# The residual of the last group on VectorE, and a new order for the last two groups

## The chip, the cores and the metric

The kernel runs on one core of a Trainium2 chip. The metric is the time of one execution on the device in microseconds (us). Five engines work side by side, each through its own list of instructions in order: TensorE (PE), VectorE (DVE), ScalarE (ACT), GpSimd (POOL), and SyncE (SP), which here does nothing but issue transfers (DMAs). A batch is one of 128 matrices of 128 x 512 float32 numbers; they are worked on in 32 groups of four, so group 31 holds batches 124 to 127.

## The reference

Two layers act on every batch `x` (128 nodes, 512 features). The names are those of the reference; `adj` is 128 x 128.

```
x = layernorm(x + max_over_features(relu(adj @ x + b)))          # layer 0
q, k, v = split(x @ w_qkv)                                       # layer 1, 8 heads of 64
attn = softmax(where(adj == 0, -inf, q @ k.T / 8))
o = (attn @ v) @ w_proj + b_proj
ln = layernorm(o) * gamma + beta
x = layernorm(x + o + ln)
```

So the last normalization works on a sum of three things: the `x` that layer 0 left, `o`, and the normalized `o`. This sum is the residual of the title.

## The kernel before, in words

The work of a batch is cut into named steps, each a small function. In the order of the data:

- `load`, `conv`, `cmax`, `bn`, `ba`, `rstdx`, `shiftx`, `norm0` and their like are layer 0. What they leave of each batch, beside the normalized `x`, is a scale and a shift per row (`c0s[b]`), from which the same `x` can be made again out of the raw input.
- `xpl` (ACT) splits `x` into two 16-bit planes, `xrow` (SP) writes them to memory as `rowsx`, and `xcross` (SP) reads them back transposed as `xT`. `xmask`, `xsub`, `xhigh` and `xd` split `xT` into the three parts `x_h`, `x_l`, `x_d`.
- `dm` and `dd` (PE) are the dense products for q, k and v of a group: the main part (L810 and L811) and the correction (L816). `main` (ACT, L835) and `rest` (DVE, L839) carry them out of PSUM, the banks that PE writes to.
- `S` (PE, L856) makes the scores, `masked` (DVE, L870) adds the mask, `rmax` takes the row maximum, `exps` (ACT, L895) the exponentials, and `recip` and `wts` (DVE) divide by the sums. `pln`, `row` and `cross` bring the weights through memory to get them transposed (`eT`); for the last group `T` (PE, L929) and `wT` (ACT, L933) do that on the chip. `AV` (PE, L942) multiplies by v.
- `omask`, `osub`, `ohigh` and `od` split the result for `po` and `pod` (PE). For the last group `ocopy` (ACT, L983) and one plain product, `po` (PE, L992), stand in their place. `pmain` (DVE, L1005 for the last group, L1009 elsewhere) and `prest` bring `o` out of PSUM.
- `sq1` (ACT, L1042) sums the squares, `st1` (POOL, L1047 and L1048) makes the standard deviation's inverse, and `sm1` (POOL, L1051) the negative mean. `n1a` (DVE, L1063) and `n1b` (DVE, L1035) are the layer norm and the sum of the three things. `sq2`, `sm2`, `st2` (with L1080), `norm2` (ACT, L1084) and `out` (SP, L1087) are the last normalization and the store.

The residual has four steps. `res` (SP, L1022) loads the raw input again into `xb`; `resx` (POOL, L1025) makes the normalized `x` by scale and shift; `resb` (POOL, L1028) adds `beta`; `reso` (POOL, L1032) adds `o`. Then `n1b` reads `xb`. In the last group three of the four `reso` (batches 125, 126 and 127) already run on DVE, by the list `tail_vector`.

The order is not that of the loops. Tables give every step of every batch a place in time: `FIRST` for the first two groups, `STEADY` with a period of 55.3 us for the groups between, `LAST` for groups 30 and 31. All steps are sorted by place, and each engine's list is what this order leaves to it. `HOMES` gives every tile its buffer, a digit per group. An engine that reaches an instruction whose data or buffer isn't ready waits there, and all that stands behind it in its list waits too. SP's transfers wait in the same way.

Of the kernel before, what the change touches and what calls it, by code (L numbers as in the profile page):

```python
# [203 lines left out]
        'load': [-109.474, -114.726, -93.981, -90.742],  # L204
        'conv': [-104.237, -98.333, -82.773, -82.116],
        'cmax': [-101.892, -96.467, -82.184, -79.932],
        'relu': [-89.028, None, -76.607],
        'bn': [-102.389, -102.929],
        'ba': [-97.381, -99.226],
        'rstdx': [-91.240],  # L210
        'shiftx': [-88.508],
        'add0': [None, None, -74.236, -75.828],
        'sq0': [None, None, -66.957, -67.365],
        'rstd0': [None, None, -63.498],
        'shift0': [None, None, 287.249],
        'norm0': [-88.385, -87.588, -62.851, -60.493],
        'xpl': [-74.327, -86.981, -61.567, -54.001],
        'xrow': [-70.245, -80.244, -61.526, -46.314],
        'xcross': [-61.792, -51.026, -55.998, -43.528],
        'xmask': [-57.244, -41.596, -45.998, -35.427],  # L220
        'xsub': [-53.734, -36.213, -41.414, -33.891],
        'xhigh': [-49.203, -38.843, -38.848, -35.169],
        'xd': [-41.803, -28.755, -12.094, -25.033],
        'dm': [23.207, 11.124, 24.535, 28.796, -12.298, -32.939, -16.991, -33.689, -11.282, -21.144, -26.452, -22.965],
        'dd': [31.731, 30.191, 42.132, 24.720, -2.046, -3.233, -1.080, -2.017, -1.075, -11.713, -8.002, -8.311],
        'main': [23.965, 11.273, 28.136, 41.632, -10.613, -28.240, -12.184, -29.670, -5.627, -19.943, -7.194, -18.020],
        'rest': [35.642, 39.477, 48.794, 42.576, -1.794, -0.009, 2.750, -0.489, 1.324, -10.598, -4.784, -1.983],
        'S': [5.191, 7.896, 15.949, 36.535],
        'masked': [8.228, 9.789, 16.156, 55.632],
        'rmax': [23.382, 10.437, 23.419, 56.699],  # L230
        'exps': [32.521, 12.027, 45.923, 65.051],
        'recip': [38.371, 27.069, 48.649, 220.318],
        'wts': [61.926, 44.590, 53.940, 639.010],
        'pln': [74.229, 47.988, 55.572, 710.492],
        'row': [77.957, 50.229, 58.332, 756.534],
        'cross': [406.710, 53.366, 62.773, 1281.945],
        'AV': [527.077, 72.876, 470.794, 1552.458],
        'omask': [705.554, 168.484, 1395.316, 1861.627],
        'osub': [969.595, 195.060, 1430.151, 1869.293],
        'ohigh': [915.589, 295.545, 1470.100, 1979.426],  # L240
        'od': [1122.692, 433.988, 1860.884, 2301.225],
        'po': [1087.408, 432.513, 1779.318, 2195.782],
        'pod': [1128.757, 532.005, 2088.953, 2473.336],
        'pmain': [1475.008, 450.218, 1861.759, 2431.202],
        'prest': [1476.096, 706.452, 2171.852, 2518.007],
        'res': [62.370, 73.327, 1281.950, 1822.046],
        'resx': [910.657, 683.370, 1423.778, 2301.220],
        'resb': [1423.773, 937.413, 1573.982, 2381.062],
        'reso': [1663.460, 980.453, 2309.512, 2854.638],
        'sq1': [1528.274, 788.799, 2263.735, 2565.873],  # L250
        'sm1': [1771.504, 991.875, 2437.789, 3063.937],
        'st1': [1705.495, 969.978, 2311.415, 3001.611],
        'n1a': [1810.676, 1060.811, 2556.983, 3097.868],
        'n1b': [1811.771, 1186.462, 2669.560, 3144.253],
        'sq2': [1974.928, 1796.303, 2685.421, 3238.046],
        'sm2': [2097.450, 1222.877, 3004.293, 3164.575],
        'st2': [2239.253, 1958.774, 3063.658, 3309.867],
        'norm2': [2258.342, 1985.361, 3244.958, 3381.155],
        'out': [2943.922, 2451.194, 3934.517, 4169.894],
    },  # L260
    -1: {
        'load': [-144.215, -122.397, -87.832, -98.818],
        'conv': [-125.843, -113.821, -74.719, -73.132],
        'cmax': [-123.821, -111.010, -74.011, -70.007],
        'relu': [-105.209, None, -68.512],
        'bn': [-132.667, -119.140],
        'ba': [-113.535, -114.070],
        'rstdx': [-105.821],
        'shiftx': [-98.066],
        'add0': [None, None, -64.370, -64.409],  # L270
        'sq0': [None, None, -58.301, -56.762],
        'rstd0': [None, None, -56.284],
        'shift0': [None, None, 38.477],
        'norm0': [-97.506, -94.514, -53.295, -51.276],
        'xpl': [-91.979, -82.995, -53.005, -42.665],
        'xrow': [-87.966, -79.711, -46.343, -37.354],
        'xcross': [-85.577, -78.906, -40.869, -29.747],
        'xmask': [-53.264, -32.333, -15.235, -20.806],
        'xsub': [-28.786, -25.524, -13.495, -17.935],
        'xhigh': [-31.154, -31.299, -15.204, -18.122],  # L280
        'xd': [-13.832, -11.080, -0.231, -7.402],
        'dm': [1471.121, 1004.949, 1170.596, 1495.141, -1.773, -8.481, 6.077, -8.919, -6.615, 11.839, 6.299, 0.944],
        'dd': [1748.325, 1492.551, 1745.786, 1001.661, 101.381, 78.388, 17.350, 78.268, 285.621, 127.289, 152.999, 16.218],
        'main': [1642.360, 1334.960, 1490.846, 1913.034, 8.547, -5.208, 12.713, -2.155, -2.160, 17.532, 11.930, 1.614],
        'rest': [2513.844, 2222.373, 1815.474, 2223.252, 273.789, 171.234, 27.561, 134.230, 319.714, 223.386, 274.327, 89.444],
        'S': [568.110, 411.072, 408.806, 560.824],
        'masked': [899.659, 650.254, 639.949],
        'rmax': [1745.444, 994.197, 1359.490, 773.421],
        'exps': [1980.015, 1064.782, 1395.489, 816.797],
        'recip': [2293.717, 1427.228, 1745.745, 1131.177],  # L290
        'wts': [2297.099, 1749.082, 1906.226, 1371.032],
        'T': [2476.054, 2147.442, 2738.042, 2147.496],
        'wT': [2625.194, 2381.724, 2922.262, 2630.593],
        'AV': [2877.033, 2419.907, 3106.656, 2910.722],
        'lp': [1372.781, 1579.539, 775.912, 1383.693],
        'ocopy': [2944.230, 2625.101, 3364.788, 3210.244],
        'po': [3112.878, 2645.586, 3631.628, 3427.698],
        'pmain': [3309.789, 2821.443, 3713.225, 3475.853],
        'res': [2527.624, 1715.942, 2450.623, 2194.028],
        'resx': [3107.444, 2037.317, 3564.952, 3402.519],  # L300
        'resb': [3572.962, 2394.415, 3628.129, 3770.640],
        'reso': [3600.985, 3042.500, 3917.033, 4144.579],
        'sq1': [3327.687, 2832.513, 3861.424, 3835.253],
        'sm1': [3694.133, 3094.171, 3933.800, 3911.237],
        'st1': [3921.399, 3009.783, 4091.118, 3870.431],
        'n1a': [3711.006, 3115.652, 4022.948, 4287.614],
        'n1b': [4022.943, 3115.693, 4144.706, 4323.473],
        'sq2': [4032.619, 3203.386, 4423.644, 4431.735],
        'sm2': [4334.289, 3281.986, 4462.030, 4479.854],
        'st2': [4341.868, 3573.354, 4467.104, 4547.705],  # L310
        'norm2': [4572.886, 3831.270, 4578.057, 4810.017],
        'out': [4797.663, 4150.269, 4805.385, 5122.998],
# [27 lines left out]
    'first_h': [0, 0, 1, 0],  # L340
}
HOMES = {
    'adjx': '0',
    'adjp': '0',
    'wr': '10--110210201210',
    'xt': [
        '02100000000000000000000000000013',
        '10321321321321321321321321321331',
        '23213213213213213213213213213223',
        '31032132132132132132132132132102',  # L350
    ],
    'pa': [
        '11001200000000000000000000000031',
        '22231200000000000000000000000032',
        '02120333333333333333333333333303',
        '10210033333333333333333333333300',
    ],
    'xm': [
        '10011111111111111111111111111110',
        '01100000000000000000000000000011',  # L360
        '10110000000000000000000000000001',
        '10001111111111111111111111111111',
    ],
    'ptx': '3203',
    'cx': '01',
# [98 lines left out]
    ],  # L464
    'pod': [
        '',
        '3020000000000000000000000000230',
        '',
        '1111111111111111111111111110002',
    ],  # L470
# [10 lines left out]
def tile_adj_resnorm_d2(  # L481
# [12 lines left out]
    nc = tc.nc  # L494
# [681 lines left out]
```

## Time and profile before

| | before |
|---|---|
| median of 3 runs | 1835.1 us (1834.6 to 1837.3) |
| time of the profiled execution | 1834.2 us |
| span of the profiled execution | 1832.4 us, TensorE clock 0.996 |
| PE busy | 1802.5 us, 98% of the span |
| DVE busy | 1526.9 us, 83% |
| ACT busy | 1549.0 us, 85% |
| POOL busy | 1288.8 us, 70% |
| last matmul ends | 1818.5 us after the span's start |

The span runs from the first to the last instruction; the profiled execution's own time is 1.8 us longer. PE's busy time is an upper bound of its work, since matmuls are pipelined and their ends are modelled; what can be read surely is where PE was idle and what it waited for.

### The profile page before, as it was taken

How to read it: one execution, taken by the hardware profiler on the slowest of the kernel's cores; microseconds unless marked ns; L12 is line 12 of the kernel's file. 1: busy time of each engine (PE TensorE's matmuls, PEld its weight loads, DVE VectorE, ACT ScalarE, POOL GpSimd, SP SyncE). 2: the span in 40 equal slices, each digit the busy share in tenths (PEclk: the TensorE clock that was granted, in tenths of full speed). 3: DMA queues.
4: the chain of work that ended last, by engine and by line, in shares of the span. 5: the costliest groups of instructions: out<-in, count | busy, mean ns of one | idle time of the engine just before them, and what ended most of it. 6: DMA issues, size and time to landing. Idle time of an engine off the chain costs nothing.

```text
span 1832.4 us, 32628 instructions
## 1 busy us (share of the span) xinstructions
PE 1802.5 (98%) x10525; PEld 1420.9 (78%) x10525; DVE 1526.9 (83%) x2539; ACT 1549.0 (85%) x3959; POOL 1288.8 (70%) x1932
## 2 busy tenths in 40 slices
PE   7999999999999999999999999999999999999996
PEld 4777777788787778787788787887877787878874
DVE  7998887888887888888888888888888888888875
ACT  5898888888888888888888988888988888878875
POOL 4166567767767767777677777677677777768878
PEclk9999999999999999999999999999999999999998
DMA  5466666667666577656576756576666676556561
GB/s 162 135 165 178 174 161 156 167 160 201 173 165 164 157 178 192 176 157 160 165 186 174 181 147 169 160 202 173 165 167 159 173 197 178 159 152 185 138 156 69
DMA packets 486715, 303.95 MB, mean 166 GB/s; under 512 B 399504, under 2 KB 403728, under 8 KB 486544
## 3 DMA queue, kind: packets, MB, share of 16 engines
q1 hardware_dynamic: 485680, 300.75, 62.1%
q8 instruction: 83, 1.36, 0.3%
q10 hardware_dynamic: 864, 1.12, 0.2%
q14 instruction: 88, 0.72, 0.1%
HBM read 73.20 MB, written 131.07 MB: 111 GB/s over the span
## 4 chain that ended last, share of the span: by engine, by line
PE 86%; POOL 6%; DVE 3%; ACT 2%; issue 1%; DMA 1%; SPq 0%; POOLq 0%; ACTq 0%; DVEq 0%
PE psc L856 7%; PE pav L942 6%; PE pa L625 5%; POOL xb L1028 1%; POOL sum L1048 1%; POOL xb L1032 1%; ACT e L895 1%; DVE o L1035 1%; POOL x_d L742 1%; POOL od L742 1%; POOL xb L1025 1%; POOL sum L1051 0%; DVE o L1063 0%; POOL sum L1047 0%; PE pv L770 0%
## 5 line engine op out<-in xcount | busy, mean ns | idle before, releaser
L895 ACT ACTIVATE e<-e,nmax 128x128 f32<-128x128 f32 x1016 | 392.6, 392 | 2.5 <-DVE nmax L878 2.4
L742 POOL TENSOR_TENSOR od<-oh,ol 128x512 fp32r<-128x512 f32 x124 | 164.4, 1326 | 132.5 <-DVE ol L960 78.4
L910 ACT COPY planes<-e 128x2048 uint16<-128x2048 uint16 x124 | 234.8, 1893 | 9.8 <-DVE e L904 6.0
L1048 POOL TENSOR_TENSOR sum<-sum,mhalf 128x1 f32<-128x1 f32 (+1 forms) x287 | 217.3, 757 | 23.9
L1032 POOL TENSOR_TENSOR xb<-xb,o 128x512 f32<-128x512 f32 x125 | 165.3, 1322 | 53.1 <-DVE o L1035 50.7
L1042 ACT ACTIVATE squares<-o,sum 128x512 uint8<-128x512 f32 x256 | 183.2, 717 | 21.5 <-DVE o L1035 15.2
L895 ACT ACTIVATION_READ_ACCUMULATOR e<-e,nmax 128x1 f32 x1016 | 194.5, 191 | 0.0
L870 DVE SCALAR_TENSOR_TENSOR e<-psc,mask 128x1024 f32<-128x1024 f32 x127 | 152.3, 1218 | 42.7 <-PE psc L856 40.6
L1028 POOL TENSOR_TENSOR xb<-xb,beta_sb 128x512 f32<-128x512 f32 x128 | 165.9, 1296 | 2.9
L904 DVE TENSOR_TENSOR e<-e,sums 128x1024 f32<-128x1024 f32 x128 | 160.7, 1256 | 1.1
L1063 DVE SCALAR_TENSOR_TENSOR o<-o,sum,gamma_sb 128x512 f32<-128x512 f32 x128 | 101.3, 791 | 69.3 <-POOL sum L1051 61.2
L878 DVE TENSOR_REDUCE nmax<-e 128x8 f32<-128x1024 f32 x127 | 152.5, 1202 | 1.0
L736 POOL TENSOR_SCALAR oh<-oxh 128x512 fp32r<-128x512 f32 x31 | 64.9, 2093 | 117.0 <-DVE oxh L732 33.3
L709 ACT COPY xplanes<-xt 128x1024 uint16<-128x1024 uint16 x124 | 129.2, 1042 | 14.0 <-DMA rowsx<-xplanes 11.3
L856 PEld LDWEIGHTS psc<-qkT 64*128 64x128 f32 x2048 | 119.5, 188 | 19.1 <-issue 17.9
L625 PE MATMUL pa<-xt,adjT 128*128 128x512 f32 x256 | 132.5, 602 | 1.5 <-DVE rm L636 1.0
L856 PE MATMUL psc<-qkT 64*128 64x128 f32 x2048 | 132.3, 279 | 0.5 <-DVE o L1035 0.5
L942 PE MATMUL pav<-eT,v 128*64 128x128 f32 x2048 | 127.1, 276 | 0.9 <-ACT eT L933 0.8
L942 PEld LDWEIGHTS pav<-eT,v 128*64 128x64 f32 x2048 | 110.4, 137 | 18.0 <-issue 9.0
L1025 POOL TENSOR_SCALAR xb<-xb,sum 128x512 f32<-128x512 f32 x128 | 115.6, 904 | 9.3 <-DMA xb<-in_x_dram 9.2
L1035 DVE SCALAR_TENSOR_TENSOR o<-o,sum,xb 128x512 f32<-128x512 f32 x128 | 98.4, 769 | 23.2 <-POOL sum L1048 18.1
L697 ACT ACTIVATE xt<-xt,sum 128x512 f32<-128x512 f32 x128 | 103.8, 813 | 12.2 <-DMA wraw<-in_L_gnn_w_qkv_dram 6.1
(4263 smaller groups left out, 5507.6 us busy)
## 6 DMA issues: line engine op xcount, KB each, us to landing
rows<-planes SPq DMA_DIRECT2D x124, 512.0 KB, 3.1
xt<-in_x_dram SPq DMA_DIRECT2D x128, 256.0 KB, 3.1
xb<-in_x_dram SPq DMA_DIRECT2D x128, 256.0 KB, 2.8
out_dram<-o SPq DMA_DIRECT2D x128, 256.0 KB, 3.2
rowsx<-xplanes SPq DMA_DIRECT2D x124, 256.0 KB, 2.5
wraw<-in_L_gnn_w_qkv_dram SPq DMA_DIRECT2D x8, 256.0 KB, 3.1
xT<-rowsx SPq DMA_TRANSPOSE x124, 3.6
eT<-rows SPq DMA_TRANSPOSE x124, 4.9
```

The source lines that it names most:

```text
L625: nc.tensor.matmul(pa[b], adjT, xs[b], start=True, stop=True)
L742: engine.tensor_tensor(d, h.bitcast(FP), l.bitcast(FP), op=ALU.subtract)
L856: nc.tensor.matmul(psc[:, s, hp, :], qkT[hs, hp, i, :], qkT[hs, KC + hp, i, :], start=not with_mask, stop=not with_mask or hp == HP - 1,)
L878: nc.vector.tensor_reduce(nmaxs[b], es[b], AX.X, ALU.max, negate=True)
L895: nc.scalar.activation(es[b][:, j, :], src[:, j, :], AF.Exp, bias=nmax[:, j : j + 1], scale=by, accum_out=sums[b][:, j : j + 1],)
L904: nc.vector.tensor_tensor(es[b], es[b], sums.pop(b)[:, :, None].to_broadcast([P, H, P]), op=ALU.mult,)
L910: nc.scalar.copy(pl, es.pop(b).rearrange("p h m -> p (h m)").bitcast(U16).rearrange("p (m s) -> p s m", s=2),)
L942: nc.tensor.matmul(pavs[b][s * HD : (s + 1) * HD, hp, :], v[:, h * HD : (h + 1) * HD], eT[:, s * HP + hp, :], start=True, stop=True,)
L1028: nc.gpsimd.tensor_tensor(xbs[b], xbs[b], beta_sb, op=ALU.add)
L1032: engine.tensor_tensor(xbs[b], xbs[b], os[b], op=ALU.add)
L1042: nc.scalar.activation(junk[:, turn[0], :], src, AF.Square, bias=s[:, 0:1], scale=-float(D), accum_out=s[:, 1:2],)
L1048: nc.gpsimd.tensor_tensor(s, s, mhalf[:, :n], op=ALU.pow)
```

## The change

For the four batches of the last group, `resx` and `reso` become one DVE operation each of the form (in0 op scalar) op in1, and `resb` is dropped for all four: `beta` goes into the first operation in place of the shift, and the shift goes into the second beside `o`. So POOL loses four `resx`, four `resb` and one `reso`, and DVE gains four `resx` and one `reso` while its other three `reso` change their form. `tail_vector` no longer decides anything.

```diff
 TWO = {
...
     'tail_vector': [0, 1, 1, 1],
...
+    'tail_fused': [1, 1, 1, 1],
 }
...
+    def fused(b):
+        return bool(TWO["tail_fused"][b % G]) and b >= B - G
+
     def resx(b):
+        if fused(b):
+            nc.vector.scalar_tensor_tensor(
+                xbs[b], xbs[b], c0s[b][0], beta_sb, op0=ALU.mult, op1=ALU.add,
+            )
+            return
         nc.gpsimd.tensor_scalar(xbs[b], xbs[b], *c0s.pop(b), op0=ALU.mult, op1=ALU.add)
 
     def resb(b):
         nc.gpsimd.tensor_tensor(xbs[b], xbs[b], beta_sb, op=ALU.add)
 
     def reso(b, vector=False):
+        if fused(b):
+            nc.vector.scalar_tensor_tensor(
+                xbs[b], os[b], c0s.pop(b)[1], xbs[b], op0=ALU.add, op1=ALU.add,
+            )
+            return
         engine = nc.vector if vector else nc.gpsimd
         engine.tensor_tensor(xbs[b], xbs[b], os[b], op=ALU.add)
```

Beside this, both tables of `LAST` have new numbers throughout (the one of group 31 has no row for `resb` any more), and the digits of `HOMES` for groups 28 to 31 are partly new. The tables of the groups before are the same. No other step's work is changed. The built programs differ from the step `load` of batch 121 on. What the new numbers do to the engines' lists, where it is more than a neighbour changing places:

| list | in the old order | in the new order |
|---|---|---|
| PE, `conv` | 122 directly before 123 | 16 dense matmuls between 123 and 122 |
| PE, group 31 | `pd` 3, main part of product 1, `po` of 120, ..., main part of product 2 | main part of product 2, `po` of 120, `pd` 3, main part of product 1 |
| PE, `AV` of 122 | after `S` of 126 and 125 | before `po` of 121 and `S` of 125 and 126 |
| ACT, end | `wT` 125, `sq1` 123, `ocopy` 125, `wT` 124, `sq2` 122, `wT` 127, `sq1` 125, `wT` 126 | `wT` 125, `ocopy` 125, `wT` 127, `wT` 124, `sq2` 122, `sq1` 123, `sq1` 125, `wT` 126 |
| DVE, after the last matmul | `pmain` 126, `reso` 126, `n1b` 124, `n1a` 126, `reso` 127, `n1b` 126, `n1a` 127, `n1b` 127 | `pmain` 126, `n1a` 124, `reso` 126, `n1b` 124, `n1a` 126, `reso` 127, `n1b` 126, `n1a` 127, `n1b` 127 |
| ACT, `xpl` of 127 | directly after `exps` of 121 | after `sq2` 115, `ohigh` 118, `norm2` 115 and one `xhigh` |
| SP, `xrow` of 127 | before `res` of 116 and `out` of 115 | after them; `xcross` of 127 before that of 126 |
| SP, `xcross` of 125 | before `cross` of 117 | after `cross` of 119 and `res` of 117 |
| SP, `load` of 125 | after `row` of 113 | before `row` of 112 |

PE's last eight steps stand in the same order in both: `po` 125, `T` 126, `AV` 124, 127 and 126, then `po` 124, 127 and 126. So do SP's last thirteen transfers.

## The prediction

> **What bounds the kernel now.** I read the page's busy shares first, then the table by stretches of the end, then the waits of PE and the order of time at the end. The page says that PE is the bound, and which POOL groups the change touches:
>
> ```profile
> PE 1802.5 (98%) x10525; PEld 1420.9 (78%) x10525; DVE 1526.9 (83%) x2539; ACT 1549.0 (85%) x3959; POOL 1288.8 (70%) x1932
> ...
> L1032 POOL TENSOR_TENSOR xb<-xb,o 128x512 f32<-128x512 f32 x125 | 165.3, 1322 | 53.1 <-DVE o L1035 50.7
> ...
> L1028 POOL TENSOR_TENSOR xb<-xb,beta_sb 128x512 f32<-128x512 f32 x128 | 165.9, 1296 | 2.9
> ...
> L1025 POOL TENSOR_SCALAR xb<-xb,sum 128x512 f32<-128x512 f32 x128 | 115.6, 904 | 9.3 <-DMA xb<-in_x_dram 9.2
> ```
>
> The table by stretches (columns: from and to, length, busy us of PE, PEld, DVE, ACT, POOL; then clock and DMA) shows that POOL, 70% busy on average, is full at the end, while PE falls silent at 1818.5:
>
> ```profile
> 1790.00:1800.00 10.00, 9.94 (x67) 8.01 (x66) 7.76 (x14) 9.07 (x28) 9.51 (x15) 1.00 0.49 159
> 1800.00:1810.00 10.00, 9.17 (x69) 5.64 (x68) 8.00 (x13) 6.28 (x12) 9.25 (x16) 1.00 0.00 1
> 1810.00:1818.50 8.50, 8.50 (x20) 3.42 (x18) 2.34 (x5) 4.51 (x10) 8.17 (x13) 1.00 0.25 93
> 1818.50:1832.40 13.90, 0.02 (x1) 0.00 (x0) 6.21 (x13) 5.48 (x11) 8.89 (x21) 0.61 0.15 57
> ```
>
> So the end has two prices: idle time of PE before 1818.5, which moves everything, and the drain of 13.9 us after it. PE's waits from 1600 on, longest first:
>
> ```profile
> PE pp_(31, 1)_19690 L810 <- DVE e L870: 1.2, 1, 1.2
> PE pav L942 <- ACT eT L933: 0.8, 2, 0.5
> PE pa L625 <- DVE rm L636: 0.8, 1, 0.8
> PE pd_(31, 6)_19480 L816 <- ACT qkT L835: 0.7, 1, 0.7
> PE pm_(29, 6)_18211 L810 <- ACT qkT L835: 0.6, 1, 0.6
> PE pd_(28, 3)_18071 L816 <- DVE v L839: 0.3, 1, 0.3
> PE pm_(29, 8)_18196 L810 <- DVE qkT L839: 0.3, 1, 0.3
> PE pd_(31, 5)_19524 L816 <- DVE qkT L839: 0.2, 1, 0.2
> ```
>
> They sum to 4.9 us: all that a better order can win on PE. In the drain, DVE's order of time (start, length, instruction, idle before) shows two losses to POOL, an n1a of 1.73 us that delays pmain of 126, and an n1b that waits for POOL's statistics:
>
> ```profile
> 1817.56 1.73 DVE L1063 SCALAR_TENSOR_TENSOR o<-o,sum,gamma_sb 128x512 f32<-128x512 f32 x1 [1.67 <-POOL sum L1051]
> 1819.21 0.68 DVE L1005 SCALAR_TENSOR_TENSOR o<-pm_('o', 126)_20078,bias_sb 128x512 f32<-128x512 f32 x1
> ...
> 1821.65 0.75 DVE L1035 SCALAR_TENSOR_TENSOR o<-o,sum,xb 128x512 f32<-128x512 f32 x1 [1.02 <-POOL sum L1048]
> ```
>
> **What the Trainium skill says.** "GPSIMD Engine Reference", Engine selection, calls an elementwise operation with two inputs about twice as slow on GpSimd; here it is 1.30 us on POOL (L1028) against 0.69 (L1032 on DVE). "SBUF — State Buffer", Terms, says that DVE and GpSimd share a port pair held exclusively for a whole instruction. The trace agrees in kind only: the n1a above took 1.73 us beside a resb, and 0.75 at 1822.33, when POOL ran only operations of one column; but the 1.0 more is less than the 1.26 of that resb, so it wasn't shut out for all of it.
>
> **The change part by part.**
>
> *Work moved.* POOL loses 4 x 0.90 + 4 x 1.30 + 1.32 = 10.1 us, nearly all between 1790 and 1819. DVE gains five operations with a scalar per row, like n1b, at 0.77 (L1063 and L1035 mean 0.79 and 0.77): 3.9 us; three reso go from 0.60 to 0.68 start to start. DVE is idle 11 of the 40 us from 1780 to 1820, so this is hidden there; with that cover gone, it costs up to 3.9. Only the two reso behind pmain 126 lie on the end's path: 2 x 0.08 = 0.2. The new resx of 125 puts a wait for xb_125 into DVE's list, ahead of v's rest; its load was issued at 1780.9 and POOL's use was at 1790.5, so I take 0.
>
> *The drain.* P is the end of the last matmul. DVE, start to start: pmain 0.61, n1a 0.66, n1b and the new reso 0.68. In the new order: 0.1 + 0.61 + 3 x 0.66 + 4 x 0.68 + 0.75 puts the end of the last n1b at P + 6.2; before, it was 1825.8, P + 7.3. POOL: n1b of 124 ends at P + 2.8, its sq2 0.9 later; st2 of 124 takes 2.0, as at 1823.84, since DVE runs beside it: P + 5.7. sm2 and st2 of 126 and of 127 take 1.4 each, as from 1825.8 to 1828.6: P + 8.5. norm2 0.8 and the rest of the store 3.0 (1829.4 to 1832.4): P + 12.3 against P + 13.9, **1.6 us**. Bounds: 0.3, if DVE's chain is slowed to the old one, and 2.6, if st2 of 124 takes 1.1.
>
> *PE's waits from 1750 on.* The wait of 1.2 was for the scores' banks: product 1 needs two banks that masked of 124 frees. Now product 2, which needs one bank, goes first (1.8 us); masked of 124 ended 2.3 us after S of 124, so 0.5 of the wait stays: gain 0.7. The 0.8 for eT: ACT stood 3.0 us at sq2 of 122, with wT of 127 behind it, because n1a of 122 waited for POOL's queue (sm1 behind resb of 123). Now wT 127 and 124 come first: gain 0.8. The 0.7 and 0.2 are for banks that a main (ACT) and a rest (DVE) must empty; the pieces and bank digits are new there, and as every main stands ahead of its bank's next user by a product or more, I take both as gone: gain 0.9. Being earlier, PE meets the next one late: wT of 125 stands behind exps of 124 (3.1 us), oh_123 and norm2 of 121; counting from there it ends 0.4 after PE could start AV of 125: -0.4. Sum **2.0 us**, bounds -1.0 (other banks late instead) and 2.9.
>
> *PE's waits from 1600 to 1750.* conv of 122 no longer follows conv of 123 into a bank that cmax must free; 3.6 us of dense work lies between: 0.8. The 0.3, 0.6 and 0.3 sit where conv 124 and 125 move; I can't tell, and take -0.2 in sum for new ones: **0.6 us**, bounds -1.5 and 2.0.
>
> *Transfers moved past others.* load of 125 now waits for its buffer ahead of row 112; the transposed read of 112 stood at 1623.7 behind loads anyway, so 0. xcross of 125 now goes at about 1714.4 and, with 3.1 us to land, is there at 1717.5; its reader was at 1721.2: 3.7 spare. xpl of 127 would end at about 1722.6; rowsx lands 2.3 later, xcross of 127 then goes at 1724.9 and that of 126 at 1726.2, landing at 1729.3; its reader (xm) was at 1731.7: 2.4 spare. I take 0; without that cover each us late is a us of PE, since x_l of the last batch ended at 1734.7, just when PE began the dense products of group 31 (1734.4).
>
> Sum: 1.6 + 2.0 + 0.6 = **4.2 us**. The profiled execution took 1834.2 (span 1832.4, 1.8 around it) and would take 1830.0. The runs' median lies 0.9 above it, so for the median I give 1835.1 - 4.2 = **1830.9**.
>
> **The rivals.**
>
> *The waits only move.* PE waits only 4.9 of 233 us; an order that clears five waits may set five others, on banks and on ACT's mains. For it: the old order too has small waits everywhere. Against: each of the three largest has a named cause that is gone. Then only the drain gains: 1833.5.
>
> *DVE becomes the bound of the drain.* Nine operations stand behind the last matmul; if three more of them lengthen as the n1a above (1.0 each), the drain gains nothing. Against: POOL's long operations are gone by then. PE's gain of 2.6 stays: 1832.5.
>
> *Slower: the x of group 31 comes late.* xrow of 127 now stands in SP's list behind res of 116, which waits until n1b of 114 frees its buffer (in the old trace it went at 1720.3, at once after that n1b). The longest wait of this kind on SP was 8.5 us. So late, x comes 8.5 - 2.4 = 6.1 us after PE wants it, the gains of the order are lost with their timing, and only 1.6 remains: 1835.1 + 6.1 - 1.6 = 1839.6. It is slower from a lateness of 2.4 + 1.6 = 4.0 us on. Against it: that n1b stands in the new DVE list only one masked later.
>
> *It does not do what it says.* The built lists show nine instructions fewer on POOL and five more on DVE, so this is out.
>
> **How the numbers follow.** 0.2% is 3.7 us, about what a measurement of this kernel can tell from no change. Forecast 0.62 (0.54 of it beyond 3.7 us, as 4.2 is not far above), waits move 0.15, DVE bound 0.10 (0.02 of it beyond), x late 0.13 (0.10 slower by over 3.7, 0.03 less late). Faster 0.56, same 0.34, slower 0.10. The likeliest case alone spans 1828.2 to 1832.9. The sum of all the good bounds is 2.6 + 2.9 + 2.0 = 7.5, which gives 1827.6, and not all come together: 1828.2 below. Above, it takes in both middle rivals and the start of the slow one: 1836.0.
>
> **What would show it.** Right: the last matmul about 2.6 us earlier; no wait of DVE for sm1 (L1051) from 1790 on; no wait of pav for eT but one of up to 0.5 at 125; pp_(31, 1) without a wait; no n1a above 1 us in the last 15 us; a drain of 12 to 12.6 us. Wrong: new waits of PE before 1755, above all dense products of group 31 waiting for x_l or x_h; xm of 126 or 127 waiting for a DMA; a drain of 13.5 or more.

## The result and the profile after

The changed kernel took 1829.64 us (median of 8 runs, 1828.21 to 1832.19), the one before 1835.28 (8 runs): a ratio of 0.997, 95% interval 0.9959 to 0.998, so 5.6 us less where 4.2 were forecast. Timed a second time, beside other kernels of this study, it gave 0.9975 (0.9964 to 0.9986), 4.6 us less. The gain is real; whether it is larger than the forecast the times leave open, since both intervals (3.7 to 7.5 and 2.6 to 6.6 us) hold 4.2. One of the 13 executions of "changed, resx doubled" in the table below ran at a granted clock of 0.247, took 6970 us and is left out; all others ran at 0.995 or more. The profiled execution of the changed kernel took 1829.64 us, with a span of 1827.8.

From the page after: the busy shares, and the three POOL groups of the residual, which have lost the last four batches (x124 where they had 125 and 128):

```profile
PE 1801.2 (99%) x10525; PEld 1421.9 (78%) x10525; DVE 1528.4 (84%) x2544; ACT 1549.0 (85%) x3959; POOL 1283.9 (70%) x1923
...
L1045 POOL TENSOR_TENSOR xb<-xb,o 128x512 f32<-128x512 f32 x124 | 160.9, 1298 | 56.9 <-DVE o L1048 54.4
...
L1036 POOL TENSOR_TENSOR xb<-xb,beta_sb 128x512 f32<-128x512 f32 x124 | 163.7, 1320 | 2.7
...
L1033 POOL TENSOR_SCALAR xb<-xb,sum 128x512 f32<-128x512 f32 x124 | 114.8, 926 | 9.6 <-DMA xb<-in_x_dram 9.5
```

The table by stretches of the end (columns as in the prediction's). The last matmul now ends at 1815.42, and POOL, nearly full in the same place before, has room:

```profile
1790.00:1800.00 10.00, 9.89 (x62) 7.18 (x61) 8.54 (x15) 7.63 (x23) 8.91 (x10) 1.00 0.37 125
1800.00:1810.00 10.00, 9.76 (x70) 5.90 (x69) 6.25 (x15) 7.80 (x17) 7.45 (x17) 1.00 0.07 27
1810.00:1815.42 5.42, 5.42 (x13) 2.10 (x11) 2.71 (x6) 2.23 (x5) 2.88 (x7) 1.00 0.26 97
1815.42:1827.85 12.43, 0.00 (x0) 0.00 (x0) 6.12 (x13) 5.48 (x11) 6.82 (x16) 0.66 0.17 64
```

PE's waits from 1600 on, all of them:

```profile
PE pav L942 <- DMA eT<-rows: 0.8, 1, 0.8
PE pm_(29, 9)_18095 L810 <- ACT qkT L835: 0.4, 1, 0.4
PE pd_(28, 3)_18073 L816 <- ACT qkT L835: 0.4, 1, 0.4
PE pd_(31, 6)_19433 L816 <- ACT qkT L835: 0.3, 1, 0.3
PE pav L942 <- ACT eT L933: 0.2, 1, 0.2
PE pav L942 <- DVE ol L960: 0.2, 1, 0.2
```

They sum to 2.3 us against 4.9. The waits for `pp_(31, 1)` and for the convolution are gone, the one for eT is down to 0.2. A wait of 0.8 for a transfer of eT is new; in the second profile of the same kernel it was 0.4, so it varies from run to run. In the drain, VectorE's order of time has no pause above 0.05 us behind its first instruction and no long instruction any more (start, length, instruction):

```profile
1815.52 0.69 DVE L1005 SCALAR_TENSOR_TENSOR o<-pm_('o', 126)_20076,bias_sb 128x512 f32<-128x512 f32 x1 [1.41 <-PE pm_('o', 126)_20076 L992]
...
1816.14 0.75 DVE L1076 SCALAR_TENSOR_TENSOR o<-o,sum,gamma_sb 128x512 f32<-128x512 f32 x1
1816.80 0.75 DVE L1040 SCALAR_TENSOR_TENSOR xb<-o,sum,xb 128x512 f32<-128x512 f32 x1
1817.46 0.75 DVE L1048 SCALAR_TENSOR_TENSOR o<-o,sum,xb 128x512 f32<-128x512 f32 x1
...
1820.92 0.75 DVE L1048 SCALAR_TENSOR_TENSOR o<-o,sum,xb 128x512 f32<-128x512 f32 x1
```

**A ruler for what follows.** Two profiles can't be compared by their spans alone: single executions of one kernel lie over some 5 us, and ahead of the end the profile after ran 1.3 us later than that of before, in a part where the two programs are the same. So I split the end at marks read from the orders of time: A, from the start of the 113th instruction `masked` on VectorE (the first of group 28; the expectations call it batch 112's, it is 114's) to that of the last one, of batch 124; B, from there to the end of the last matmul; C, the drain. Before, the marks are 1595.20, 1774.38, 1818.52 and 1832.42; after, 1596.48, 1772.89, 1815.42 and 1827.85. Behind the last `masked` both have the same work for PE. One thing the marks do not share: in the four profiles of the old order the last `masked` starts 1.1 us after PE has ended its scores, in the ten of the new order 0.5 us after it (the reason is shown under the prediction's points). So between the two orders 0.6 us of what A falls belongs, for PE, to B. All kernels of this study:

| kernel | A | B | C | B + C | ratio to before (95%) |
|---|---|---|---|---|---|
| before | 179.2 | 44.1 | 13.9 | 58.0 | |
| changed, two profiles | 176.4, 175.7 | 42.5, 42.5 | 12.4, 12.4 | 55.0, 55.0 | 0.997 (0.9959 to 0.998), 0.9975 (0.9964 to 0.9986) |
| order alone, two | 176.3, 176.1 | 43.6, 43.6 | 15.3, 15.3 | 58.9, 59.0 | 1.0002 (0.9993 to 1.001), 0.9995 (0.9987 to 1.0003) |
| residual alone, two | 177.9, 179.4 | 44.8, 45.0 | 12.3, 12.3 | 57.2, 57.3 | 0.9997 (0.9988 to 1.0005), 0.9998 (0.999 to 1.0005) |
| order, only 125 fused | 177.1 | 42.9 | 15.5 | 58.4 | 0.9995 (0.9987 to 1.0004) |
| order, all but 125 fused | 176.3 | 43.6 | 12.4 | 56.0 | 0.9981 (0.9974 to 0.9988) |
| before, two waits attacked | 178.2 | 45.0 | 14.4 | 59.4 | 1.0007 (0.9999 to 1.0015) |
| changed, tail pulled | 175.2 | 42.5 | 11.5 | 54.0 | 0.9971 (0.9962 to 0.9981) |
| changed, tail ordered | 177.7 | 43.2 | 10.7 | 53.8 | 0.9966 (0.9954 to 0.9979) |
| changed, resx doubled | 178.1 | 44.0 | 12.4 | 56.5 | 0.9974 (0.9964 to 0.9984) |
| changed, reso doubled | 176.9 | 42.5 | 13.9 | 56.4 | 0.9977 (0.9969 to 0.9985) |

B + C repeats within about 0.1 us where a kernel was profiled twice; of before there is one profile. A varies by over 1 us: 177.9 to 179.4 in the four profiles of the old order (mean 178.7), 175.2 to 178.1 in the ten of the new one (mean 176.6). So the new order is worth about 2.1 us in A, with or without the new residual; 0.6 of them are the shift of the mark, and about 1.5 are PE's.

### The profile page after: what moved, and what is told of

Read it like the earlier page. It is cut to its first block, busy times and chain, and to the rows that moved or that the text cites. A ratio compares the mean times of both kernels' runs of the same rounds, so it can differ in the third digit from the quotient of the medians.

```text
span 1827.8 us, 32614 instructions
## 1 busy us (share of the span) xinstructions
PE 1801.2 (99%) x10525; PEld 1421.9 (78%) x10525; DVE 1528.4 (84%) x2544; ACT 1549.0 (85%) x3959; POOL 1283.9 (70%) x1923
## 5 line engine op out<-in xcount | busy, mean ns | idle before, releaser
L1055 ACT ACTIVATE squares<-o,sum 128x512 uint8<-128x512 f32 x256 | 183.1, 717 | 21.8 <-DVE o L1048 15.8
L1045 POOL TENSOR_TENSOR xb<-xb,o 128x512 f32<-128x512 f32 x124 | 160.9, 1298 | 56.9 <-DVE o L1048 54.4
L904 DVE TENSOR_TENSOR e<-e,sums 128x1024 f32<-128x1024 f32 x128 | 159.9, 1250 | 1.1
L1076 DVE SCALAR_TENSOR_TENSOR o<-o,sum,gamma_sb 128x512 f32<-128x512 f32 x128 | 99.2, 775 | 64.3 <-POOL sum L1064 57.2
L709 ACT COPY xplanes<-xt 128x1024 uint16<-128x1024 uint16 x124 | 129.2, 1042 | 14.4 <-DMA rowsx<-xplanes 12.2
L697 ACT ACTIVATE xt<-xt,sum 128x512 f32<-128x512 f32 x128 | 103.9, 813 | 12.4 <-POOL sum L691 10.0
```

The lines of the kernel that those rows point to most:

```text
L904: nc.vector.tensor_tensor(es[b], es[b], sums.pop(b)[:, :, None].to_broadcast([P, H, P]), op=ALU.mult,)
L1045: engine.tensor_tensor(xbs[b], xbs[b], os[b], op=ALU.add)
L1055: nc.scalar.activation(junk[:, turn[0], :], src, AF.Square, bias=s[:, 0:1], scale=-float(D), accum_out=s[:, 1:2],)
```

## The experiments

### The two halves alone

Order alone: the tables and homes of the changed kernel, the residual of before.

```
-    'tail_fused': [1, 1, 1, 1],
+    'tail_fused': [0, 0, 0, 0],
...
         'resx': [3353.537, 2093.860, 3785.974, 3547.076],
+        'resb': [3353.541, 2093.865, 3785.976, 3547.080],
```

> The new order with the old residual: the tables and homes of after, with the last four batches' residual as before (resx and resb on GpSimd, resb put directly behind resx; reso on GpSimd for 124, on VectorE for the other three). My theory, two parts that add: PE keeps its part (last matmul about 4.4 us earlier than before, counted from the masked instruction of batch 112), but the drain is as before or longer, 13.9 to 14.5 us against 12.4 in after, because POOL again has four operations of 0.9 and four of 1.3 between the statistics: about 1831.3 us, 1.7 above after. Rival, the order gives everything: 1829.6, as after. Rival, the relief of POOL gives most: 1834 or more, with DVE waiting for POOL's sm1 and PE waiting again before 1815.

Residual alone: the tables and homes of before, with the new functions.

```
+    'tail_fused': [1, 1, 1, 1],
...
-        'resb': [3572.962, 2394.415, 3628.129, 3770.640],
```

> The new residual in the old order: the tables and homes of before without the row resb of the last group, and the fused resx and reso on VectorE. My theory: PE waits as before (four or five waits, 4 to 5 us from 1600 on, pp_(31, 1) and pav for eT among them), the drain falls from 13.9 to 12.4 to 12.9 us, because n1a of 124 no longer waits for POOL's queue and no longer lasts 1.73 us: about 1834.0 us, 1.3 less than before. Rival, the order gives everything: 1835.3. Rival, the relief of POOL gives most: 1831.5 or less, with the waits of PE after 1790 gone too.

Each was timed twice. The expectations of the second time:

> The order alone, a second time. The times said 0.1 us more than before, the trace said 2.0 less (PE's stretch 3.4 shorter, drain 1.4 longer). If the trace stands for the kernel, the ratio is about 0.999 (1833.1) and PE's stretch is again 218 to 220.5; if the times do, 1.000 and a stretch nearer 222. The waits of 0.6 at pd_(o, 123) for POOL's od and of 0.7 at pav for eT, and a drain of about 15.4, should come back in either case.

> The residual alone, a second time: ratio 0.9992 (1833.5), since the drain is 1.5 us shorter (12.3 to 12.4) and PE's stretch is that of the old order, 222.7 to 223.3. If the times of the first measurement were right at 0.9 us less, the same within their error.

Neither half showed what I expected of it. The order alone was 0.4 us slower and 0.9 faster than before (ratios times 1835) where I expected 4.0 faster; the residual alone was 0.6 and 0.4 faster where I expected 1.3, which its intervals still hold. No interval leaves 1 out. The changed kernel is 5.5 and 4.6 faster. My theory of two parts that add is refuted by the order alone, and so is the rival that the order gives everything. The rival that the relief of POOL gives most was right for the order alone (1834 or more, with PE waiting again) and wrong for the residual alone (1831.5 or less). Of the second expectations, the order alone met that of its trace (PE's stretch A + B 219.7, both waits back); the residual alone had a stretch of 224.3, longer than the 222.7 to 223.3 expected.

B + C and A together show where the two parts interlock. In B + C, from 58.0, the residual alone takes 0.8, the order alone adds 0.9, and both together take 3.1; A's 2.1 for the order come on top. This makes 0.8 for the residual, 1.2 for the order and 5.2 for both. That fits the times but for the order alone, which they put at 0.3 on average. Of this difference 0.2 lies outside the span (its executions took 2.0 us around the span, those of before 1.8); the rest is within what A's spread allows and was not settled.

What holds the order back shows in its waits. From the view of PE's waits of the order alone, from 1773 on:

```profile
PE pav L943 <- ACT eT L934: 0.7, 1, 0.7
PE pd_('o', 123)_19922 L817 <- POOL od L743: 0.6, 1, 0.6
```

and from its order of time on VectorE at the end:

```profile
1815.68 0.69 DVE L1006 SCALAR_TENSOR_TENSOR o<-pm_('o', 127)_20068,bias_sb 128x512 f32<-128x512 f32 x1 [3.79 <-DMA out_dram<-o]
...
1819.15 0.69 DVE L1006 SCALAR_TENSOR_TENSOR o<-pm_('o', 126)_20080,bias_sb 128x512 f32<-128x512 f32 x1 [2.77 <-DMA out_dram<-o]
...
1822.47 0.75 DVE L1049 SCALAR_TENSOR_TENSOR o<-o,sum,xb 128x512 f32<-128x512 f32 x1 [1.35 <-POOL sum L1062]
```

The last matmul ended at 1817.96, but pmain of 126 started 1.2 us later (0.1 in the changed kernel), because the buffer of `o` that it writes was still being stored: with POOL's statistics behind the residual, norm2 and the stores of the earlier batches are late (the last two norm2 ahead of the last matmul's end started 5.3 and 1.8 us before it, 6.7 and 4.8 in the changed kernel). And n1b waits another 1.35 for POOL. This makes the drain 15.3.

### Which batch's residual costs what

From the changed kernel; the diff is that of the first run, and the second has the flags 1, 0, 1, 1 and a place of `resb` for 125 alone.

```
-    'tail_fused': [1, 1, 1, 1],
+    'tail_fused': [0, 1, 0, 0],
...
+        'resb': [3353.541, None, 3785.976, 3547.080],
```

> The new order; the new residual for batch 125 alone, the other three as before on GpSimd. In the order alone, PE waited 0.6 us at pd_(o, 123) for od of 123, which stood on POOL behind resb of 125 (2.1 us), and the drain was 15.3. Theory: the parts interlock at two places, POOL ahead of 1800 (batch 125, PE's part) and POOL behind 1808 (124, 126, 127, the drain). Then PE's stretch from the masked instruction of batch 112 to the last matmul falls from 219.9 to about 219 us, and the drain stays at 15 or so: about 1.0 us less than the order alone. Rival, only the amount of POOL's work counts: both fall a little, the drain to about 14.5.

> The counterpart: the new order; the new residual for 124, 126 and 127, batch 125 as before on GpSimd. Theory: PE's stretch as in the order alone, 219.9 us with its wait of 0.6 at pd_(o, 123), and the drain as in the changed kernel, 12.4: about 1.0 us above the changed kernel. Rival, only the amount counts: PE's stretch 219.2, drain 13.1.

The changed kernel ran beside them:

> The changed kernel again, unchanged, beside the next three on one chip. The order alone and the residual alone, timed together, gave 0.1 more and 0.9 us less than before; the change as a whole had given 5.6 less in another session. If the two parts need each other, it gives 5 to 6 less here too: 1829.6. If that figure owed something to its session, 2 to 3 less.

It gave 4.6 less (by the ratio), between the two branches of its expectation and nearer the first. The theory of two places holds in B and C. In A + B the run with 125 alone fused missed it (220.0 where about 219 was expected), with a wait of 1.9 us in A, at `po` of 118 for an n1b, that no other profile has. With 125 on GpSimd the drain is that of the changed kernel (12.4), and PE's waits behind the last `masked` are again just these two:

```profile
PE pav L943 <- ACT eT L934: 0.7, 1, 0.7
PE pd_('o', 123)_19922 L817 <- POOL od L743: 0.6, 1, 0.6
```

With 125 alone fused the second is gone, the first falls to 0.2, and the drain stays at 15.5. So batch 125's two POOL operations cost PE 1.1 us (B, 43.6 against 42.5). Both waits come out of POOL's list. The od of 123 stands behind the two operations: it ended 21.8 us after the start of the last `masked` in the order alone, 20.0 after it in the changed kernel. And the last wT stands on ACT behind squares that wait for an n1b, whose n1a waits for POOL's reso: with 125 on GpSimd that n1b came 1.2 us later than in the changed kernel. The operations of 124, 126 and 127 cost 2.9 to 3.1 us of drain, and with 125 alone fused B is still 42.9, as `po` of 126 starts 0.4 late behind ACT's oxh. The rival, that only the amount counts, gave a drain between the two in both runs; neither showed one.

### What sets the drain

Changed kernel, order of the end alone: `st1` of 124 behind its `sm1`; `n1a`, `n1b` of 124 (and in the second run `reso`, `n1a` of 127) ahead of pmain of 126; resx of 126, the statistics, squares, norm2 and stores are moved along. The diff is of the first version and cut to two rows; the second has n1a of 127 at 3812.600.

```
-        'n1a': [3877.907, 3291.580, 4309.470, 4559.968],
+        'n1a': [3812.400, 3291.580, 3850.000, 3840.000],
-        'n1b': [4302.225, 3324.051, 4356.434, 4579.296],
+        'n1b': [3812.420, 3324.051, 3851.000, 3842.000],
...
```

> After, with only the end of the order changed: st1 of 124 directly behind sm1 of 124 on POOL, and n1a, reso and n1b of 124 behind pmain of 127 on VectorE, so that six of its operations stand behind the last matmul instead of nine; statistics, squares, norm2 and stores follow in the order 124, 127, 126. If VectorE's chain behind the last matmul sets the drain, as the prediction's sum has it, the last n1b comes about 1.5 us earlier (last matmul + 4.7 instead of + 6.25) and the drain falls from 12.4 to about 10.9 us: 1828.1 us. If POOL's chain of statistics or the stores set it, the drain stays at 12 to 12.4: 1829.6. If the n1a of 124 holds up pmain of 127 or 126, it is longer.

In this first version reso of 124 and 127 read `o` after n1a had overwritten it, so for these two batches another residual is added; the instructions are as many and as long. The second version keeps the arithmetic:

> The changed kernel with a shorter drain, by order alone and with the same arithmetic: st1 of 124 behind its sm1 on POOL; on VectorE reso of 124 ahead of pmain of 127, then n1a and n1b of 124, reso and n1a of 127, so that only pmain of 126, n1b of 127, reso, n1a and n1b of 126 stand behind the last matmul, five operations in place of nine. If VectorE's chain sets the drain: last n1b at about last matmul + 4.0, drain 10.2 to 11.0 us against 12.4, and about 1.5 to 2 us less than the changed kernel, 1827.8. If POOL's statistics of 126 or the stores do, the drain stays above 11.8.

And the reverse, two more operations behind the last matmul:

```
+            if b >= B - 2:
+                nc.vector.scalar_tensor_tensor(
+                    xbs[b], xbs[b], 1.0, beta_sb, op0=ALU.mult, op1=ALU.add,
+                )
```

> The changed kernel with a second operation of the same form behind the fused reso of 126 and of 127 (it adds beta once more): two more of VectorE's operations behind the last matmul, eleven instead of nine. If VectorE's chain sets the drain, it grows by 2 x 0.66 = 1.3 us to 13.7 and the last n1b comes at last matmul + 7.6. If POOL's chain has slack or sets it, the drain grows by less than 0.7.

In the changed kernel VectorE's chain sets it, and POOL's statistics run level with it. Two operations more made the drain 13.9, 1.45 longer (0.73 each), with the last n1b ending 7.7 us after the last matmul instead of 6.25. In the first version two fewer, not three, stand behind the last matmul (seven; the expectation counted six): the drain was 11.5, 0.95 shorter. In the second, four fewer made it 10.7, 1.76 shorter, and the last n1b came 1.76 earlier too. That is less than four times 0.68: pmain of 126 starts 0.26 late behind n1a of 127, n1a of 126 pauses 0.13 behind its own reso, and the last n1b waits for the next limit, POOL's st1 of 126 (VectorE's order of time of the tail ordered):

```profile
1819.17 0.75 DVE L1048 SCALAR_TENSOR_TENSOR o<-o,sum,xb 128x512 f32<-128x512 f32 x1 [0.46 <-POOL sum L1061]
```

Both orders also take statistics of 124 on POOL out of the drain. That POOL has to be shortened along with VectorE shows in the residual alone. Its VectorE chain ends 5.7 us after the last matmul, 0.5 sooner than in the changed kernel, and the drain is 12.3 all the same: there POOL's statistics run with no pause above 0.1 us from 0.9 after the last matmul to the last st2, 8.5 after it.

The tail ordered has the lowest ratio of the study, 0.9966 against 0.9975 of the changed kernel beside it; the intervals overlap, so that it is the better one is shown by its drain, not by the times. Its B was 0.6 longer, with waits of pav for eT of 0.7 in sum that the edit wasn't to touch; their cause stays open.

### Is VectorE's added work hidden?

```
             nc.vector.scalar_tensor_tensor(
                 xbs[b], xbs[b], c0s[b][0], beta_sb, op0=ALU.mult, op1=ALU.add,
             )
+            nc.vector.scalar_tensor_tensor(
+                xbs[b], xbs[b], 1.0, beta_sb, op0=ALU.mult, op1=ALU.add,
+            )
```

> The changed kernel with a second operation of the same form behind each of the four fused resx on VectorE (it adds beta once more): 4 x 0.68 to 0.75, about 2.8 us more on VectorE, all ahead of the last pmain. The prediction took VectorE's five added operations as hidden. If so, no change: the drain stays at 12.4 us and PE's stretch from the masked instruction of batch 112 to the last matmul stays within what its repeats show, 217.7 to 220.9; time as the changed kernel, 1830 to 1831. If VectorE has no slack there, up to 2.8 us more, with PE waiting for VectorE behind 1790.

Only partly. C is unchanged, but B grew from 42.5 to 44.0, and PE's waits behind the last `masked` name VectorE:

```profile
PE ppt L929 <- DVE o L1051: 1.0, 1, 1.0
PE ppt L929 <- DVE e L904: 0.5, 1, 0.5
```

They sum to the 1.5. So the slack there is about half of the 2.8 us added. (PE's stretch A + B was 222.2, above the 220.9 that the expectation allowed; the rest of that lies in A.) The times (4.8 less than before, as the changed kernel) can't tell 1.5 us.

The residual alone points the same way in the old order: its B is 0.7 to 0.8 longer than before's, with a new wait of 1.2 of `pm_('o', 125)` for ACT's oxh. The traces show what held that oxh up. The new resx of 125 puts a `wts` (L904) on VectorE 0.7 us later, and this changes which of two operations starts first, it or a reso on POOL. Before, then the residual alone:

```profile
1795.28 1.22 DVE L904 TENSOR_TENSOR e<-e,sums 128x1024 f32<-128x1024 f32 x1
1795.33 2.32 POOL L1032 TENSOR_TENSOR xb<-xb,o 128x512 f32<-128x512 f32 x1
```

```profile
1792.58 1.28 POOL L1045 TENSOR_TENSOR xb<-xb,o 128x512 f32<-128x512 f32 x1
1792.84 2.10 DVE L904 TENSOR_TENSOR e<-e,sums 128x1024 f32<-128x1024 f32 x1
```

Before, VectorE was 0.05 us ahead and POOL's reso lasted 2.32; now POOL was ahead and `wts` lasted 2.10 instead of 1.22. So 0.7 us of added work became 1.6 us at pmain of 123, 1.4 at the prest of 123 behind it (counted from the last `masked`), and `sq1` of 123, which waits for that, stands ahead of `ocopy` of 125 on ACT.

### Two waits taken out of the old order

```
-        'dm': [1471.121, 1004.949, 1170.596, 1495.141, ...],
+        'dm': [1471.121, 1170.596, 1004.949, 1495.141, ...],
...
-        'wT': [2625.194, 2381.724, 2922.262, 2630.593],
+        'wT': [2625.194, 2381.724, 2922.262, 2629.000],
```

> Before, with two small edits of its order and nothing else: product 2 of group 31 changes places with product 1 (so the one that needs a single bank comes first), and wT of 127 goes ahead of sq2 of 122 on ACT. They aim at the two longest waits of PE at the end, 1.2 us at pp_(31, 1) and 0.8 at pav for eT. If each wait costs what the view of waits shows less the 0.5 that I left standing, the time falls by 1.5 us to 1833.8; if a wait costs PE more than its idle time (start to start, those places stood 1.39 and 1.27 us above the usual pace), by 2.0 to 2.6: 1833.0. Rival, the waits only move: 1835.3, with new waits of the same sum in the view of waits.

The rival was right here, and the loss was larger still in the profile: B grew by 0.9 and the drain by 0.5. From its waits of PE, from 1776 on:

```profile
PE pp_('o', 120)_19700 L810 <- POOL od L742: 1.4, 1, 1.4
PE pav L942 <- ACT v L835: 0.9, 1, 0.9
PE pav L942 <- ACT eT L933: 0.7, 2, 0.4
```

The wait of `pp_(31, 1)` went, and `po` of 120, now straight behind product 2, waited 1.4 for od of 120 in its place. The two for eT stayed at 0.7 in sum, and one for v came. With these two edits alone the waits moved; the new order took `pp_(31, 1)` out and left 0.2 for eT by moving the rest as well (`pd` 3 now stands behind the main part of `po` 120, for one).

## Why the prediction was right, point by point

**Drain, 1.6 forecast: 1.5 measured, twice.** The steps were right one by one: last n1b at last matmul + 6.2 (6.25), st2 of 124 at + 5.7 (5.5), st2 of 127 at + 8.5 (8.6), end at + 12.3 (12.43). Two chains met on the way: POOL was through with st2 of 124 and sm2 of 126, over which the sum goes, at 1821.12, and sq2 of 126, behind VectorE's n1b of 126, ended at 1821.13. What it gave to the new order here isn't its own: the old order with the new residual has 12.3.

**PE's waits from 1750 on, 2.0, and from 1600, 0.6.** By the ruler B fell by 1.6 and A by about 2.1, in sum 3.7 against 2.6. With the mark's 0.6 us put where PE spends them, B fell by 2.2, where the terms that lie in it (0.7 + 0.8 - 0.4) made 1.1, and A by about 1.5, where 0.9 + 0.6 made 1.5. So the shortfall lies in B. First, no wait of 0.5 stayed at po of 120. I took `masked` of 124 to end 2.3 us after S of 124; it ended 1.7 after it. The reason is VectorE's instruction between the two (before, then after):

```profile
1773.70 0.76 DVE L883 TENSOR_SCALAR nmax<-nmax 128x8 f32<-128x8 f32 x1
1774.38 1.21 DVE L870 SCALAR_TENSOR_TENSOR e<-psc,mask 128x1024 f32<-128x1024 f32 x1
```

```profile
1772.81 0.17 DVE L883 TENSOR_SCALAR nmax<-nmax 128x8 f32<-128x8 f32 x1
1772.89 1.22 DVE L870 SCALAR_TENSOR_TENSOR e<-psc,mask 128x1024 f32<-128x1024 f32 x1
```

Before, it ran beside a reso on POOL (1773.15 to 1774.44) and ended 0.03 after it; after, that reso was over. Second, I priced each wait at its idle time. Start to start, the nine waits of before stand 6.5 us above the usual pace of their matmuls, where the view sums them to 4.9: `pp_(31, 1)` 1.39 for 1.2, the two for eT 1.27 for 0.8, the convolution 0.95 for 0.8. The third guess, 0.4 of new wait at AV of 125, was one of 0.2 at AV of 126, 0.5 start to start. The terms of B then read 1.1 + 0.5 + 0.7 - 0.1 = 2.2, as measured. That A meets its 1.5 is in part luck: it varies by over 1 us, and a wait of 0.4 to 0.8 for a transfer came that I had not forecast.

**VectorE's 3.9 us as hidden: half right.** Ahead of the last matmul the new order had made the room, but only that much: doubled, four of them cost 1.5, and in the old order B grew by 0.7 to 0.8 with them, through the order in which VectorE and POOL started. The price that I named for the case that the cover is gone was the right kind of answer; that it is nearly gone I did not see, because I read VectorE's idle time (11 of 40 us) as if it lay where it was needed.

**The two parts added up: wrong in form, though not in sum.** I summed drain and waits as if either half could be had alone. Alone they give about 1 us or less each. That the sum came near is luck in this respect: the change brought both parts, so nothing in its time could tell a sum from an interlock.

**The n1a of 1.73 us: read wrongly.** The prediction took it as shut out for a part of POOL's resb only, since it was 1.0 longer and the resb 1.26. But the resb had begun 0.08 us earlier:

```profile
1817.48 1.26 POOL L1028 TENSOR_TENSOR xb<-xb,beta_sb 128x512 f32<-128x512 f32 x1
```

When n1a began, 1.18 of it were left, and n1a ended 0.55 after it. The last section shows that this is a whole block.

**The rivals.** "The waits only move" was right for the two edits in the old order and wrong for the whole. "VectorE bounds the drain" was right that it is the bound (POOL's statistics run level with it), wrong that its operations would lengthen: none took more than 0.75. "x of group 31 comes late" did not happen: the last transposed read was issued at 1727.2, the last two took 3.5 from issue to landing (median), its reader started at 1732.4, so 1.7 us were left where I had 2.4. That it becomes slower from 4.0 us of lateness on was not tried.

**What would show it.** The signs listed as right came: no wait of VectorE for sm1, pp_(31, 1) without a wait, no long n1a in the last 15 us, a drain of 12.43. The last matmul is 3.1 us earlier, and 4.4 counted from the 113th `masked`. One sign listed as wrong came too, new waits of PE before 1755: 0.8 at 1672 for a transfer of eT (0.4 in the second profile), 0.4 at pm_(29, 9) and 0.2 at 1717. It was drawn too wide: all waits from 1600 to 1755 still fell, from 2.7 to 2.0. Its main case, group 31 waiting for x_l or x_h, did not come.

## What to carry to other kernels

Where two engines' queues cross in a kernel's last stage, price operations and order together: here each alone was worth under 1 us by the times, and both 5. Compare profiles by stretches between marks that all versions share, since the spans of single executions scatter by more than such a change is worth. And behind the last matmul count the operations of the engine whose chain runs without a gap; each one added cost its start-to-start time here (0.73), each one moved ahead won about two thirds of it (0.44 to 0.48), as the next engine's chain soon took over.

## What was not expected of the hardware

An operation of VectorE on 128 x 8 numbers, the one shown above, took 0.73 to 0.76 us in all four profiles of the old order, beside a POOL operation on 128 x 512, and ended 0.02 to 0.03 us after it; in all ten of the new order it ran without one and took 0.17. The n1a and n1b behave alike where their big inputs are in SBUF: in the profile of before all seven that began while such a POOL operation had run for 0.07 us or more (with over 0.25 left) ended 0.54 to 0.55 us after it, whatever was left of it (0.38 to 1.20). That agrees with what the Trainium skill says of the shared port pair ("SBUF — State Buffer", Terms): it is held for the full instruction, and the loser is fully blocked. Not every operation is: in the same place 183 operations of VectorE that read PSUM took 0.63 to 0.69 as elsewhere, and 36 reciprocals on 128 x 8 took 0.17 to 0.20. In the cases shown here the loss fell on the engine that started second, and a shift of 0.3 us moved a loss of 0.9 or 1.0 us from one engine to the other, as the two pairs of lines with `wts` show.

POOL's operations of one column took 0.19 and 0.57 us alone and up to 0.66 and 0.95 beside VectorE in the drain of the changed kernel; a chain of statistics on POOL is priced by what VectorE does meanwhile.
